# q and k stored whole and parted by GpSimd in attention's first chunk, with three edits in the last layer

## The chip, the cores and the metric

The kernel runs on one core of one Trainium2 chip. The core has TensorE (matrix products; PE in the profile), VectorE (DVE), ScalarE (ACT), GpSimd (POOL) and SyncE (SP), which here only issues transfers. Each takes its own instructions in order; they wait for one another through semaphores. The metric is the device time of one launch in microseconds. Times "at" a number are counted from the start of the profiled span.

## The reference

A graph network of four layers on 3327 nodes with 128 features, and a random adjacency matrix of zeros and ones with about 16 neighbours per node. Every layer computes `x = x + layer(relu(layernorm(x)), adj)`:

- Layer 0: two rounds of `swish(adj @ h @ W + b)`.
- Layer 1: attention with 128 heads of 8 numbers each. q, k and v are raw reshapes of `h @ W.T` to (128, 3327, 8), so that one head's 3327 x 8 numbers come from about 26 consecutive nodes. The scores are `q k.T * 128**-0.5 + 2 adj`, then a softmax over the 3327 columns, the product with v, and an output projection.
- Layer 2: `relu(adj @ h @ W_msg)` through a gated recurrent cell.
- Layer 3: `z = leaky_relu(lap(adj, h) @ W1 + b1)`; all 3327 x 3327 squared distances between rows of z; for every row, the four nearest get `exp(-distance / 2)` added to the adjacency, and `lap(adj', h) @ W2 + b2` is the output, where `lap(A, x) = d * (A @ (d * x))`, d the inverse square root of the row sums.

## The kernel before, in words

Nodes lie on 128 partitions, 26 to a partition (N = 3327 nodes, T = 26, padded to NP = 3328). A matrix of nodes is walked in T tiles of 128 rows.

**Projection (lines 376 to 445).** After the layernorm and 26 transposes, a loop over r takes 128 nodes at a time: six products of 128 x 512 give 1024 numbers of q, k and v. For q and k, ScalarE writes the high part, the value rounded to the short fp32r format (L409), VectorE writes what is left over, the low part (L410), and takes the largest absolute value (L411). High and low part lie side by side in the tile `qk_st`, and SyncE stores both into the DRAM tensors `qt` and `kt`, whose 16 rows are 8 rows of high and 8 rows of low parts (L412). v is stored with a column of ones into `vd` (L419). At r == 1 the heads of group 0 are loaded (L421). Stores, loads and buffers in this part are ordered by the scheduler of the tile framework.

**Attention (lines 466 to 564).** The columns are cut into 7 chunks of 476 (`QW`), and the 128 heads into 32 groups of 4. The work is written out by hand as 7 x 32 x 26 steps (`manual_schedule`): every engine, SyncE included, takes its instructions in the order in which the steps issue them. A step t of a group does, in this order:

- `scores` (L483): four products of 32 x 128 by 32 x 476, one per head on its own row group of TensorE; to some heads the adjacency is added on VectorE (L499), to one on TensorE (L497), and in odd steps one head is taken without it, `exp` on ScalarE (L500) and then multiplied on GpSimd by `exp` of the adjacency (L502). In odd steps ScalarE takes the exponential of the five other results of the pair (L504).
- `weigh` (L506) of the step four before (`ahead = 4`): products with v, summed over the steps in one PSUM bank; at the end of a group the sum is copied (L520) and stored (L523).
- at t == 4, `load_heads` (L346) for the next group: 28 transfers on SyncE, 8 of keys into the one buffer `k_in` (`bufs=1`), 16 of queries, 4 of values.
- from t == 13, `key_pair` (L368): GpSimd copies the keys of two tiles into the order that TensorE reads.
- at t == 22, the adjacency tile of the next chunk: a load on SyncE and a doubling on GpSimd (L270), and a store of an older one (L481).

**After attention: `tail` (lines 586 to 829).** Output projection; `adj_product` for layer 2 in 26 tiles (L228, three bf16 parts of y on TensorE; the adjacency tiles `a16` are loaded from `adj16` through a pool opened for each product); the gates; `adj_product` for layer 3, z and its norms; then for each of 26 tiles the distances: 14 instructions of fp32 products (L774), 7 products of three rows that add the other rows' norms (L777), ScalarE's copy with the own norm (L778), VectorE's eight largest values and their places (L779, L780). `second` (L749) turns these into weights in pieces of 4, 9 and 13 tiles. While the third `adj_product` runs, `gather` (L787) fetches for each tile the four nearest rows of y from DRAM, one indirect transfer of GpSimd each, 104 in all, and VectorE weighs and adds them (L798, L800); TensorE transposes the sums (L805). At the end the product and the gathered sums are multiplied by W2 (L822, L823), scaled, added to x and stored.

At the very end a loop that runs `n_gen` times, 0 or 1, holds a general path for inputs on which the fast path isn't safe. `n_gen` is computed after the projection.

Of the kernel before, what the change touches and what calls it, by code (L numbers as in the profile page):

```python
# [8 lines left out]
F32 = mybir.dt.float32  # L9
F32R = mybir.dt.float32r  # L10
# [10 lines left out]
P = 128  # L21
# [5 lines left out]
E = 8  # L27
# [26 lines left out]
def kernel(  # L54
# [56 lines left out]
    deg = const.tile([P, T], F32, name="deg")  # L111
    a_max = const.tile([P, T], F32, name="a_max")
# [21 lines left out]
    def in_pieces(f):  # L134

        todo = [slice(t0, t1) for t0, t1 in zip(CUTS, CUTS[1:]) if t1 > t0]

        def done(t):
            while todo and todo[0].stop <= t:
                p = todo.pop(0)  # L140
                f(p, p.stop - p.start)

        return done
# [47 lines left out]
    def adj_matmul(agg, lhs, on_tile=None, bufs=3):  # L191

        cs = chunks(N, 512)
        with tc.tile_pool(name="adj_ps", bufs=1, space=PSUM) as ps, tc.tile_pool(name="adj_in", bufs=bufs) as ap:
# [23 lines left out]
    def adj_matmul_parts(agg, parts, on_tile=None):  # L218

        cs = chunks(N, 512)  # L220
        with tc.tile_pool(name="adj_ps", bufs=1, space=PSUM) as ps, tc.tile_pool(name="adj_in", bufs=4) as ap:
            acc = [ps.tile([P, 512], F32, name=f"agg_ps{c}") for c in range(len(cs))]
            for t in range(T):
                a = ap.tile([P, N], BF16, name="a16")
                nc.sync.dma_start(a, adj16[t])
                for i, part in enumerate(parts):
                    for c, (c0, w) in enumerate(cs):
# [5 lines left out]
                            stop=(t == T - 1 and i == 2),  # L233
# [39 lines left out]
    with tc.tile_pool(name="l0", bufs=1) as pool:  # L273
# [46 lines left out]
        fix = pool.tile([P, 1], F32, name="fix")  # L320
        nc.gpsimd.affine_select(fix, ones, pattern=[[0, 1]], compare_op=ALU.is_gt, fill=0.0, base=P - 1, channel_multiplier=-1)
        nc.vector.tensor_scalar(fix, fix, -1.0, 1.0, op0=ALU.mult, op1=ALU.add)
        nc.vector.tensor_add(deg[:, T - 1 : T], deg[:, T - 1 : T], fix)
# [4 lines left out]

    kt = dpool.tile([HL, GP], F32, name="kt")
# [15 lines left out]

    def load_heads(c, g):  # L346
        q0, _ = q_chunks[c]
        we = even(c)
        k_in = kq.tile([P, NP], F32, name="k_in", bufs=1)
        q4 = kq.tile([P, QW], F32R, name="q4")  # L350
        v4 = kq.tile([P, 4, T, EA], F32, name="v4")
        for i in range(4):
            n0 = (4 * g + i) * N
            for j in range(2):
                r = 32 * i + HL * j
                nc.sync.dma_start(k_in[r : r + HL], kt[:, n0 : n0 + NP])
                for k in range(2):
                    nc.sync.dma_start(
                        q4[r + E * k : r + E * k + E, :we].bitcast(F32),
                        qt[E * j : E * j + E, n0 + q0 : n0 + q0 + we],  # L360
                    )
# [14 lines left out]
    with tc.tile_pool(name="l1", bufs=1) as pool, tc.tile_pool(name="l1_ps", bufs=3, space=PSUM) as ps:  # L376
# [6 lines left out]
        for tail in (qt, kt):  # L383
            nc.gpsimd.dma_start(tail[:, N * NH :], zero)
# [12 lines left out]
        assert 3 * N + NP <= P * NH  # L397
        for r in range(T):
            kp = rows_of(r)
            lhs = hT[:, r * P : r * P + kp]  # L400
            for i, (dst, mx) in enumerate(((qt, q_max), (kt, k_max))):
# [3 lines left out]
                scale = D**-0.5 if i == 0 else 1.0  # L405
                s = st.tile([P, 2, E * NH], F32R, name="qk_st")
                full = pp[:kp].rearrange("p a b -> p (a b)")
                hi = s[:kp, 0].bitcast(F32)
                nc.scalar.activation(s[:kp, 0], full, AF.Copy, scale=scale)  # L409
                nc.vector.scalar_tensor_tensor(s[:kp, 1], full, scale, hi, op0=ALU.mult, op1=ALU.subtract)  # L410
                nc.vector.tensor_reduce(mx[:kp, r : r + 1], hi, AX.X, ALU.max, apply_absolute_value=True)  # L411
                store(dst.rearrange("e (r c) -> r e c", c=NH), s.bitcast(F32).rearrange("p a (e c) -> p (a e) c", c=NH), r, kp)  # L412
# [7 lines left out]
            if r == 1:  # L420
                first = load_heads(0, 0)  # L421
                while len(first[3]) < T // 2:
                    key_pair(first)
                e_first = [exp_of(a, 0) for a in a_first[1::2]]
# [15 lines left out]
        general = pool.tile([P, 1], F32, name="general")  # L440
# [515 lines left out]
```

## Time and profile before

| what | us |
| --- | --- |
| median of 3 runs | 11397.28 (11396.15 to 11406.29) |
| the profiled execution | 11392.72 |
| its span, first to last instruction | 11391.0 |
| layer 0 and layernorm, 0 to 382 | 382 |
| projection, to the first group's start at 641 | 259 |
| attention, 641 to 10592 | 9951 |
| output projection, to 10687 | 95 |
| layer 2, to 10861 | 174 |
| layer 3, first product, to 10974 | 113 |
| z and norms, to 11007 | 33 |
| distances, to 11215 | 208 |
| last weights, second product and gathers, to 11360 | 145 |
| last products and output, to 11391 | 31 |

The stages are cut at instructions in the order of time; the rows from 0 to 11391 sum to the span. A line of a timeline gives the start, the duration, the engine, the line of the code, the operation, output and inputs, and how many instructions were merged; in brackets stands how long the engine stood idle before it and what released it. A group line gives the count, then the busy time and the mean of one in ns, then the idle time just before, by releaser. A line of stretches gives start and end, the length, busy time and count of PE, PEld (weight loads), DVE, ACT and POOL, the granted clock of TensorE, the share of the DMA engines' time, and GB/s.

### The profile page before, as it was taken

What the parts mean: (1) busy time and instruction counts of PE and PEld (TensorE: products, weight loads), DVE (VectorE), ACT (ScalarE), POOL (GpSimd) and SP (SyncE); (2) the same over time, 40 slices, a digit from 0 to 9 for tenths busy, and PEclk for the clock granted to TensorE, in tenths of its full rate; (3) what the DMA queues carried; (4) which work ended last, traced back from release to release, by engine and by line L of the source; (5) the groups of instructions that cost most, each with busy time, mean ns of one, the idle gap of its engine ahead of it and who ended that gap; (6) DMA issues with size and microseconds to landing.
All of it is one profiled execution on the core that took longest, in us unless ns stands there. A gap on an engine that the chain in (4) does not pass through costs nothing. (4 is left out here: it accounts for less than half of the span.)

```text
span 11391.0 us, 212068 instructions
## 1 busy us (share of the span) xinstructions
PE 11065.1 (97%) x80100; PEld 3098.6 (27%) x80100; DVE 9408.1 (83%) x15508; ACT 10238.7 (90%) x9182; POOL 5727.5 (50%) x6218
## 2 busy tenths in 40 slices
PE   9789999999999999999999999999999999999998
PEld 4322222222222222222222222222222222222554
DVE  8678888888888888888888888888888888888555
ACT  0379999999999999999999999999999999999332
POOL 0135555555555555555555555555555555555103
PEclk9899999999999999999999999999999999999999
DMA  7853444444444444444444444444443434444423
GB/s 268 244 122 60 70 62 67 64 62 69 61 69 63 63 68 61 69 63 63 67 61 69 63 61 67 61 68 63 62 68 60 68 57 58 58 57 59 138 79 114
DMA packets 476579, 889.80 MB, mean 78 GB/s; under 512 B 91863, under 2 KB 423112, under 8 KB 439962
## 3 DMA queue, kind: packets, MB, share of 16 engines
q1 hardware_dynamic: 470952, 864.64, 43.5%
q8 instruction: 633, 10.37, 0.5%
q0 software_dynamic: 4592, 11.50, 0.3%
q14 instruction: 402, 3.29, 0.1%
HBM read 763.30 MB, written 112.46 MB: 77 GB/s over the span
## 5 line engine op out<-in xcount | busy, mean ns | idle before, releaser
L499 DVE TENSOR_TENSOR p<-early,a 128x476 f32<-128x476 f32 (+1 forms) x14560 | 8435.6, 644 | 1419.7 <-PE early L494 1192.3
L504 ACT ACTIVATE p<-p 128x2380 f32<-128x2380 f32 (+1 forms) x2912 | 6757.4, 2321 | 14.2 <-DVE p L499 0.5
L511 PE MATMUL acc<-p,v 128*9 128x476 f32 (+1 forms) x46592 | 5879.6, 564 | 33.4 <-POOL p L502 13.6
L502 POOL TENSOR_TENSOR p<-p,e 128x476 f32<-128x476 f32 (+1 forms) x2912 | 3539.2, 1215 | 3296.0 <-ACT p L500 3259.4
L500 ACT ACTIVATE p<-late 128x476 f32<-128x476 f32 (+1 forms) x5824 | 4529.2, 897 | 38.9 <-DMA vd<-v_st 20.3
L494 PE MATMUL early<-q,k 32*128 32x476 f32 (+1 forms) x14560 | 2882.9, 477 | 18.8 <-DVE p L499 18.8
L494 PE MATMUL late<-q,k 32*128 32x476 f32 (+1 forms) x8736 | 2797.3, 478 | 62.7 <-ACT p L500 36.3
L373 POOL CAST k<-k_in 128x256 fp32r<-128x256 f32 x2912 | 1946.7, 703 | 1162.5 <-DMA q<-qt 582.7
L494 PEld LDWEIGHTS late<-q,k 32*128 32x128 f32 x8736 | 1065.4, 181 | 4769.9 <-ACT p L500 3241.0
L497 PE MATMUL late<-a,two_i 128*128 128x476 bf16 (+1 forms) x5824 | 2181.0, 374 | 0.0
L494 PEld LDWEIGHTS early<-q,k 32*128 32x128 f32 x14560 | 1144.9, 181 | 23.9 <-DVE p L499 19.5
L511 PEld LDWEIGHTS acc<-p,v 128*9 128x9 f32 x46592 | 710.6, 88 | 1406.4 <-issue 1185.1
L497 PEld LDWEIGHTS <-two_i 128*128 128x128 bf16 x5824 | 556.3, 96 | 1327.5 <-issue 1327.5
L187 ACT COPY agg<-agg_ps 128x512 f32<-128x512 f32 x15 | 8.2, 590 | 476.7 <-PE agg_ps L201 289.7
L228 PE MATMUL agg_ps<-a,part 128*128 128x512 bf16 (+1 forms) x1638 | 338.0, 368 | 18.1 <-DMA a<-adj 13.7
L270 POOL TENSOR_SCALAR a<-a_in 128x476 bf16<-128x476 f32 (+2 forms) x156 | 222.2, 1424 | 0.5
L228 PEld LDWEIGHTS <-part 128*128 128x128 bf16 x1638 | 161.7, 99 | 188.6 <-DVE d_half L759 13.7
L409 ACT ACTIVATE qk_st<-pp 128x1024 fp32r<-128x1024 f32 (+1 forms) x52 | 53.3, 1024 | 149.0 <-DMA qt<-qk_st 67.4
L270 POOL TENSOR_SCALAR a<-a 128x476 bf16<-128x476 f32 (+1 forms) x26 | 36.4, 1400 | 295.3 <-DMA a<-in_adjT_dram 295.3
L778 ACT ACTIVATE dist<-sp,nsq 128x2048 f32<-128x2048 f32 (+1 forms) x52 | 85.5, 1647 | 109.8 <-PE sp L777 100.8
L774 PE MATMUL sp<-yT,hT 128*128 128x512 f32 (+1 forms) x364 | 168.2, 603 | 3.6 <-ACT hT L726 2.1
L201 PE MATMUL agg_ps<-a,h 128*128 128x512 f32 (+2 forms) x364 | 147.4, 568 | 24.3 <-DVE h L162 24.3
(192 smaller groups left out, 2520.2 us busy)
## 6 DMA issues: line engine op xcount, KB each, us to landing
k_in<-kt SPq DMA_DIRECT2D x1792, 208.0 KB
v<-vd SPq DMA_DIRECT2D x896, 117.0 KB
a<-in_adjT_dram SPq DMA_DIRECT2D x50, 1663.5 KB
a<-adj SPq DMA_DIRECT2D x78, 831.8 KB
q<-qt SPq DMA_DIRECT2D x3072, 14.9 KB
a_in<-in_adjT_dram SPq DMA_DIRECT2D x125, 238.0 KB
qt<-qk_st SPq DMA_DIRECT2D x25, 1024.0 KB
kt<-qk_st SPq DMA_DIRECT2D x25, 1024.0 KB
```

Of the source, the lines that this page charges most:

```text
L201: nc.tensor.matmul(acc[c][:, :w], lhs[:kp, t, :], a[:kp, c0 : c0 + w], start=(t == 0), stop=(t == T - 1))
L228: nc.tensor.matmul(acc[c][:, :w], part[:, t, :], a[:, c0 : c0 + w], start=(t == 0 and i == 0), stop=(t == T - 1 and i == 2),)
L270: nc.gpsimd.tensor_scalar(a2[:kp, :w], a, 2.0, None, op0=ALU.mult)
L373: nc.gpsimd.tensor_copy(k, slots(k_in)[:, t : t + 2, :])
L494: nc.tensor.matmul(sp[:, :we], pairs[t // 2][r, t % 2, :], q4[r, :we], start=True, stop=ways[i] != "I")
L497: nc.tensor.matmul(late[:, i - n_d, :we], two_i, a2[:, :we], start=False, stop=True)
L499: nc.vector.tensor_tensor(p8[:, places[i], :we], early[i][:, :we], a2[:, :we], op=ALU.add)
L500: nc.scalar.activation(p8[:, places[n_d] : places[3] + 1, :we], late[:, :, :we], AF.Exp)
L502: nc.gpsimd.tensor_tensor(p8[:, places[3], :we], p8[:, places[3], :we], e_a[:, :we], op=ALU.mult)
L504: nc.scalar.activation(p8[:, :5, :we], p8[:, :5, :we], AF.Exp)
L511: nc.tensor.matmul(acc[32 * i : 32 * i + EA, :w], v4[:kp, i, t, :], p8[:kp, PLACES[t % 2][i], :w], start=(t == 0), stop=(t == T - 1),)
L774: nc.tensor.matmul(sp[:, c0 : c0 + w], slots(zT)[:, t, :], z2T[:, cols], start=True, stop=False)
```

## The change

- In the projection q and k are stored whole, one 1024-column tile `qk_st` each, into new tensors `qf` and `kf`. The low part on VectorE is gone.
- A class `Parting` makes the two parts of a group's k and q. For each side it loads the four heads' numbers as 96 partitions of 1109 columns into `lo_k` or `lo_q`; `part` then lets GpSimd, in four pieces of 278 columns, cast them to fp32r into a tile named `hi` and subtract that in place from the loaded tile; `store` writes both into `kt` or `qt`. Groups 0 and 1 are parted inside the projection, one item of a list `early` per row r; `load_heads(0, 0)` is moved from r == 1 into that list, behind them. From there on group g of the first chunk parts group g + 2: the k side in steps 2 to 5 with its store at step 7, the q side in steps 9 to 12 with its store at step 14; the loads for group g + 3 are at step 20.
- `load_heads` loads N columns of keys and w of queries and clears the padding by a memset on GpSimd.
- Layer 3: `h @ W2` is computed beside the first product (`project_quad`), and y is made from it, so that the last product needs no weights but only transposes. The nearest row of the four is taken from y in place, not gathered, and the gathered sum is added straight to x. Whether the nearest row was each row itself is checked on VectorE and joins `n_gen` at the end. The norm products use four row groups (rows 0, 32, 64, 96) in turn. The adjacency pool stays open over all products; the distance tiles use the buffers `ln_xc` and `agg`. `second` has a fourth piece: 4, 9, 9 and 4 tiles.
- The general path reads `kf` and `qf` instead of adding the parts.

```diff
+    JW = 12
+    WJ = 4 * N // JW
+    W4 = -(-WJ // 4)
+    SIDES = ((kf, kt, "lo_k"), (qf, qt, "lo_q"))
+    class Parting:
+        def __init__(self, g):
+            self.g, self.hi, self.lo = g, [None] * 2, [None] * 2
+        def rows(self, ap, r):
+            return dram(ap, r * GP + 4 * self.g * N, [[GP, E], [WJ, JW], [1, WJ]])
+        def load(self, side):
+            src, _, name = SIDES[side]
+            self.lo[side] = kq.tile([E * JW, WJ], F32R, name=name, bufs=1)
+            nc.sync.dma_start(self.lo[side].bitcast(F32), self.rows(src, 0))
+        def part(self, side, i):
+            if i == 0:
+                self.hi[side] = kq.tile([E * JW, WJ], F32R, name="hi", bufs=1)
+            p = slice(i * W4, min((i + 1) * W4, WJ))
+            hi, lo = self.hi[side][:, p], self.lo[side][:, p]
+            nc.gpsimd.tensor_copy(hi, lo.bitcast(F32))
+            nc.gpsimd.tensor_sub(lo, lo.bitcast(F32), hi.bitcast(F32))
+        def store(self, side):
+            dst = SIDES[side][1]
+            nc.sync.dma_start(self.rows(dst, 0), self.hi[side].bitcast(F32))
+            nc.sync.dma_start(self.rows(dst, E), self.lo[side].bitcast(F32))
+        def at(self, t):
+            for side, t0 in ((0, 2), (1, 9)):
+                if t0 <= t < t0 + 4:
+                    self.part(side, t - t0)
+                if t == t0 + 5:
+                    self.store(side)
...
-                s = st.tile([P, 2, E * NH], F32R, name="qk_st")
-                full = pp[:kp].rearrange("p a b -> p (a b)")
-                hi = s[:kp, 0].bitcast(F32)
-                nc.scalar.activation(s[:kp, 0], full, AF.Copy, scale=scale)
-                nc.vector.scalar_tensor_tensor(s[:kp, 1], full, scale, hi, op0=ALU.mult, op1=ALU.subtract)
-                nc.vector.tensor_reduce(mx[:kp, r : r + 1], hi, AX.X, ALU.max, apply_absolute_value=True)
...
+                s = st.tile([P, E * NH], F32, name="qk_st")
+                nc.scalar.activation(s[:kp], pp[:kp].rearrange("p a b -> p (a b)"), AF.Copy, scale=D**-0.5 if i == 0 else 1.0)
+                nc.vector.tensor_reduce(mx[:kp, r : r + 1], s[:kp], AX.X, ALU.max, apply_absolute_value=True)
+                store(dst[:E].rearrange("e (r c) -> r e c", c=NH), s.rearrange("p (e c) -> p e c", c=NH), r, kp)
...
                 if t == min(4, T // 2) and more:
                     coming = load_heads(*groups[n])
+                if c == 0 and g + 2 < n_groups:
+                    if t == 0:
+                        parting = ahead_part
+                    for due in range(t, t + 1 if t < T - 1 else max(T, 21)):
+                        parting.at(due)
+                        if due == 20 and g + 3 < n_groups:
+                            ahead_part = Parting(g + 3)
+                            ahead_part.load(0)
+                            ahead_part.load(1)
...
+                            r = slice(c0 // 16, c0 // 16 + 3)
-                            nc.tensor.matmul(sp[:, c0 : c0 + w], one_rows, n_rows[:, cols], start=False, stop=True)
+                            nc.tensor.matmul(sp[:, c0 : c0 + w], one_rows[r], n_rows[r, cols], start=False, stop=True)
...
+                    if k == 0 and not general:
+                        row = y[:, t, :]
+                    else:
+                        row = gpool.tile([P, D], F32, name="row")
...
-                        nc.tensor.matmul(op[:, j, :], slots(agg)[:, t0 + j, :], w2_s, start=True, stop=False)
-                        nc.tensor.matmul(op[:, j, :], gT[:, t0 + j, :], w2_s, start=False, stop=True)
+                        nc.tensor.transpose(op[:, j, :], slots(agg)[:, t0 + j, :], ident)
```

## The prediction

> **What bounds the kernel now.** I read first the page's forty slices and its costliest groups: from 641 to 10592 us the span is attention, 224 groups of 26 steps (7 chunks of columns by 32 groups of four heads). Then I read the order of time of each engine in a few groups of the first chunk, and the busy times of the stages around it.
>
> ```profile
> L504 ACT ACTIVATE p<-p 128x2380 f32<-128x2380 f32 (+1 forms) x2912 | 6757.4, 2321 | 14.2 <-DVE p L499 0.5
> L502 POOL TENSOR_TENSOR p<-p,e 128x476 f32<-128x476 f32 (+1 forms) x2912 | 3539.2, 1215 | 3296.0 <-ACT p L500 3259.4
> L373 POOL CAST k<-k_in 128x256 fp32r<-128x256 f32 x2912 | 1946.7, 703 | 1162.5 <-DMA q<-qt 582.7
> ```
>
> ScalarE sets the pace: it is hardly ever idle, and two steps take 3.385 us (26 steps, 44.0 us). TensorE is close behind (1.64 us a step, 3.28 a pair). GpSimd looks half empty, and its long idle times are waits, for ScalarE and, at L373, for transfers. The order of time of one group (step 0 near 730.7 us) shows why:
>
> ```profile
> 738.04 1.38 SPq L523 DMA_DIRECT2D ot<-o  x4
> 739.52 0.33 SPq L356 DMA_DIRECT2D k_in<-kt  x1
> ...
> 755.39 0.32 SPq L356 DMA_DIRECT2D k_in<-kt  x1
> ...
> 757.22 0.35 SPq L362 DMA_DIRECT2D v<-vd  x1
> 757.86 0.35 SPq L481 DMA_DIRECT2D adj<-a  x1
> ```
>
> ```profile
> 748.03 1.22 POOL L502 TENSOR_TENSOR p<-p,e 128x476 f32<-128x476 f32 x1 [2.17 <-ACT p L500]
> ...
> 754.80 1.21 POOL L502 TENSOR_TENSOR p<-p,e 128x476 f32<-128x476 f32 x1 [2.17 <-ACT p L500]
> 761.50 1.35 POOL L373 CAST k<-k_in 128x256 fp32r<-128x256 f32 x2 [5.50 <-DMA q<-qt]
> 762.77 1.25 POOL L502 TENSOR_TENSOR p<-p,e 128x476 f32<-128x476 f32 x1
> ```
>
> ```profile
> 756.30 0.98 PE L511 MATMUL acc<-p,v 128*9 128x476 f32 x8
> ...
> 763.06 1.98 PE L511 MATMUL acc<-p,v 128*9 128x476 f32 x8
> ```
>
> The 28 transfers of `load_heads`, written at step 4, hold SyncE's queue from 739.5 to 757.6, some 18 us or eleven steps; even the adjacency store written at step 22 goes out at 757.86, the moment the queue is free. GpSimd takes its work in order too: at step 13 it waits until 761.5 for the keys, 6.1 us after the last key transfer was issued, and the product of step 15 comes late, so that TensorE's `weigh` at 763.06 takes 1.98 us for 0.98. That costs next to nothing, as TensorE runs some 2 us ahead of ScalarE. (Step 15's scores are at 755.57; the `weigh` at 756.30 is that of step 11, four steps back.)
>
> Before attention, the projection is bound by transfers, at 301 GB/s with the DMA engines full:
>
> ```profile
> 428.00:620.00 192.00, 134.22 (x256) 49.22 (x256) 101.25 (x88) 65.27 (x66) 11.16 (x28) 0.91 1.04 301
> ```
>
> **The change part by part.** All sums stand against the profiled execution, 11392.7 us (span 11391.0); the median shown, 11397.3, is 4.6 above it.
>
> *Projection, q and k stored whole: -50 us.* A row takes 8.97 us for 1024 + 1024 + 576 KB; without the low parts it is 1600 KB, 5.46 us at the same rate, while TensorE needs 12 x 0.43 = 5.15 and ScalarE 3 x 1.02. 26 rows x 3.5 = -91. Added there: the parting of groups 0 and 1 (0.85 MB loaded, 1.70 stored, each) and the first loads of group 2, 6.0 MB or 20 us. GpSimd's four partings (8 instructions of 0.72 = 5.8 us a side, priced below) are waited for on SyncE, with the row stores behind them: from nothing, if the backlog covers them, to 4 x (5.8 + 6.1 for a landing) = 47. I take 20, nearer the lower end, because backlog stands at every row. The removed L410 (52 x 1.22 on VectorE) is worth nothing: transfers cover it. Bounds -80 to -20.
>
> *First chunk, parting on GpSimd: +371 us.* Price of one: a cast of 278 columns by L373 (0.67 us for 256 when back to back) is 0.73, a subtraction by L502 (1.21 for 476) 0.71; a side is 4 of each, 5.75 us, a group 11.5. As work that fits: GpSimd is busy 25 of 44 us. The order does not fit. Both sides write their high part to the one buffer named `hi` (`bufs=1`), so the first cast of the q side, at step 9, has to wait until the k side's `hi` has been stored and has landed. That store is written at step 7, behind `load_heads` of step 4 on SyncE's queue. Its data are ready early (steps 2 to 5, done near 745), but the queue is free only at 757.6. The landing: 6.1 us for a key transfer of 208 KB in that backlog, so 416 KB issued at 758 is there near 763.5. Meanwhile GpSimd, in order, stands from 749.25 (product of step 9 done) to 763.5. Behind the waiting cast are the two partings of steps 9 and 10 (2.9 us) and then the product of step 11: done at 767.6. TensorE wants it at 756.3 and stands 11.3 us; with it stand VectorE and ScalarE, which empty what is begun. The product of step 13 follows two more partings, at 771.7; after that GpSimd catches up (2.55 us a pair against 3.385).
>
> What the group loses: TensorE resumes at 767.6. With its usual durations ScalarE takes up step 20 near 778.1 instead of 766.53. It will not have its usual clock: after the 19 us idle before 641 its scores take 0.76 us for 0.48 and the first 44 us have a granted clock of 0.86 against 1.00 later. About 5 us of such work adds 1.5. So 13.1, less 0.3 that the wait at step 13 costs now: 12.8 a group. Group 0 is spared (its loads start before its first step), groups 30 and 31 part nothing: 29 x 12.8 = 371. From both sides: with the smallest landing shown (2.4 us, from the last `nd` store to the load that waits on it) plus 1.5 for 416 KB at 301 GB/s the cast starts at 761.9, 11.2 a group, 325; with a landing of 10 at 768, 17, 495. SyncE's later work (the q side's stores wait for GpSimd until about 771, then the next loads, then the adjacency tile of step 22, due near 780) still comes in time; if it did not, the slack is TensorE's four steps, 6.7 us.
>
> The Trainium skill, in "DMA: Bandwidth & Descriptors", section "Anatomy of one DMA", puts a transfer at about 2.0 us fixed plus bytes by 436 GB/s. By that rule the store would be there 3.0 us after issue, at 761, a group would lose about 10.3, and the sum would be lower by 73. The trace's 6.1 us under backlog is what I use, since this store goes out behind the same backlog.
>
> The cut of `k_in` to N columns and two memsets of one column (0.13 us): nothing, in GpSimd's idle time; without that cover 224 x 0.13 = 29 us of GpSimd.
>
> *Tail: -37 us.* (a) h w2 beside layer 3's first product: TensorE fills that product (111.8 of 113 us), so 26 transposes (0.11 each, L646) and 52 matmuls (0.234, L718) add +15. (b) Norm rows on four row groups: a distance tile takes TensorE 7.82 us, of it 1.03 + 0.71 for L777; in parallel some 0.5 (attention's four row-group scores end 0.49 us after they begin), and VectorE's 3.63 + 0.09 + 3.62 = 7.36 with a small gap becomes the bound: 26 x 0.46 = -12, +2 for the small instructions of a fourth piece. (c) The last piece is 4 tiles for 13: gathers start 4 us earlier. (d) 78 gathers for 104 at 1.249: -32. TensorE's last product (111.7) then becomes late next; it starts after the last distance tile, as its adjacency tiles are loaded ahead and the first pieces are ready. (c) and (d) together -33, at worst -20 if TensorE starts as late as now (11219.4). (e) Last stage: 26 transposes of 0.23 for 104 matmuls of 18.8 us in all; VectorE's 9.3 us takes over, -9. The reduction for `need` falls beside the output. Bounds -50 to -15.
>
> Sum: 11392.7 - 50 + 371 - 37 = 11676.7; against the median, about 11680 us.
>
> **The rivals.** (1) *The wait is hidden.* GpSimd's own work is short, and half its time is free; if the high part is free again by step 9, only gains are left: 11397 - 87 = 11310. For it: the data are ready 4 us before step 9. Against: eleven steps of queue. It decides where a group loses less than 87 / 29 = 3.0 us, so where the k side's store has landed by 753.7, before the last of the head loads is even issued. (2) *The wait is longer.* The k store writes the tensor that `load_heads` reads; if it waits also for those reads (761.5) it lands near 767: +3.5 x 29, 11780. Against: in the projection a row store goes out at 420.90, 0.2 us after the last such load was issued. (3) *Half of it.* Fewer bytes in the queue or a short landing, 4 to 8 us a group: 11450 to 11540. (4) *The nearest row is not the row itself* somewhere: then the general branch repeats attention, more than double the time; a row's distance to itself is zero but for rounding, so under 1%.
>
> **How the numbers follow.** Forecast 0.65 (its own range 11570 to 11780), (1) 0.13, (2) 0.12, (3) 0.09, mixtures within 0.2% 0.01. For the range I leave out (1) below and a little above: 11440 to 11820. Faster by over 0.2% is (1), 0.13; within 0.2%, about what a measurement can tell from no change, 0.02; slower 0.85.
>
> **What would show it.** GpSimd's cast of the parting with some 14 us idle before it, 29 times, ended by a `kt` store; TensorE's L511 waiting for the product of step 11, 11 us each; groups of the first chunk near 57 us, those of later chunks at 44; attention starting near 590 for 641; gathers 78, distance tiles at 7.4. I am wrong if the parting's store reaches the queue ahead of the loads, if the two sides hold separate buffers, or if the first chunk's groups stay at 44 us.

## The result, and the profile after

The kernel after takes 11738.8 us (median; 11715.3 to 11741.2) against 11401.8 for the kernel before, run beside it (11396.2 to 11406.6). The ratio is 1.0291, with a 95% interval from 1.0273 to 1.0309: slower, by 337 us. The profiled execution took 11737.6 us, span 11735.8, which is 344.8 more than the span of before. Those 344.8 us can be laid out by stage, each time read from the order of time of the two traces:

| stage | before | after | difference | forecast |
|---|---|---|---|---|
| start to the output store of the first group | 694.1 | 627.1 | -66.9 | -50 |
| first output store to the end of attention | 9898.1 | 10261.9 | +363.7 | +371 |
| end of attention to the end | 798.8 | 846.8 | +48.0 | -37 |

The two large terms came as forecast. The third has the wrong sign, and most of the experiments below were spent on it.

**First chunk.** The page's costliest groups of the kernel after show the new wait and the two engines that wait with it (busy time, mean ns of one, then the idle time before it and what ended it):

```profile
L567 PE MATMUL acc<-p,v 128*9 128x476 f32 (+1 forms) x46592 | 5929.0, 566 | 333.0 <-POOL p L558 312.7
L556 ACT ACTIVATE p<-late 128x476 f32<-128x476 f32 (+1 forms) x5824 | 4511.6, 891 | 384.1 <-PE late L553 371.5
L377 POOL CAST hi<-lo_q 96x278 fp32r<-96x278 f32 (+1 forms) x128 | 52.6, 413 | 426.6 <-DMA kt<-hi 397.5
```

Ahead of the 128 casts of the q side GpSimd stood idle 397.5 us for the landing of a store from `hi`; TensorE stood 312.7 us for GpSimd's products, and ScalarE 371.5 us for TensorE. In the order of time this wait stands before the first q cast of each of groups 1 to 29, 13.8 to 15.4 us each. One group gives the chain. First SyncE's queue (start, duration, what is issued):

```profile
1023.29 1.38 SPq L579 DMA_DIRECT2D ot<-o  x4
1024.77 0.31 SPq L405 DMA_DIRECT2D k_in<-kt  x1
...
1042.40 0.36 SPq L411 DMA_DIRECT2D v<-vd  x1
1043.05 0.71 SPq L382 DMA_DIRECT2D kt<-hi  x1
1044.33 0.66 SPq L383 DMA_DIRECT2D kt<-lo_k  x1
1054.25 0.64 SPq L382 DMA_DIRECT2D qt<-hi  x1
```

The k side's store goes out at 1043.05, the moment the last head load is issued; its data had been ready since 1028.3, as GpSimd's order of time shows:

```profile
1027.90 0.42 POOL L377 CAST hi<-lo_k 96x275 fp32r<-96x275 f32 x1
1028.40 0.77 POOL L378 TENSOR_TENSOR lo_k<-lo_k,hi 96x275 fp32r<-96x275 f32 x1
1029.88 1.22 POOL L558 TENSOR_TENSOR p<-p,e 128x476 f32<-128x476 f32 x1 [0.71 <-ACT p L556]
1033.27 1.22 POOL L558 TENSOR_TENSOR p<-p,e 128x476 f32<-128x476 f32 x1 [2.17 <-ACT p L556]
1049.04 0.41 POOL L377 CAST hi<-lo_q 96x278 fp32r<-96x278 f32 x1 [14.55 <-DMA kt<-hi]
...
1051.48 1.18 POOL L558 TENSOR_TENSOR p<-p,e 128x476 f32<-128x476 f32 x1
```

The q side's first cast waits 14.55 us until that store has landed, 6.0 us after its issue, and the product of step 11 comes at 1051.48, behind two pairs of casts and subtractions. TensorE is ready for it at 1042.5:

```profile
1041.54 0.98 PE L567 MATMUL acc<-p,v 128*9 128x476 f32 x6
1052.71 1.75 PE L567 MATMUL acc<-p,v 128*9 128x476 f32 x2 [10.19 <-POOL p L558]
1054.40 0.76 PE L550 MATMUL late<-q,k 32*128 32x476 f32 x1
```

Here one sees the stop (10.19 us) and the low clock behind it (0.76 us for 0.48; the granted clock from 1053 to 1057 is 0.57, and 1.00 again from 1057). Groups 1 to 29 take 56.5 us on average, 55.5 to 57.7, for 44.3 before, which is 355 us of the 363.7. From group 30 on a group takes 44.45 us for 44.41, which is the other 8.

**Tail.** From the end of attention the stages moved by +3.1 (output projection), +0.8 (layer 2's product), +15.8 (layer 3's first product, with h w2 beside it: 127.6 for 111.8), -9.2 (distances, 207.6 for 216.8), **+42.5** (from the end of the last FIND, VectorE's last search for the nearest rows, to TensorE's first instruction of the last stage: 190.0 for 147.5) and -4.3 (last stage); the rest is -0.6. The +42.5 is in TensorE's order of time in the last product:

```profile
11513.70 33.75 PE L232 MATMUL agg_ps<-a,part 128*128 128x512 bf16 x167 [1.43 <-ACT agg L879]
11548.29 0.27 PE L232 MATMUL agg_ps<-a,part 128*128 128x255 bf16 x1 [0.83 <-issue]
11551.07 0.38 PE L232 MATMUL agg_ps<-a,part 128*128 128x512 bf16 x1 [2.51 <-issue]
11553.88 0.59 PE L232 MATMUL agg_ps<-a,part 128*128 128x512 bf16 x1 [2.44 <-issue]
11556.67 0.58 PE L232 MATMUL agg_ps<-a,part 128*128 128x512 bf16 x1 [2.20 <-issue]
...
11640.89 69.39 PE L232 MATMUL agg_ps<-a,part 128*128 128x512 bf16 x336 [0.35 <-issue]
```

For 34 us the product runs at its full rate. Then a matmul comes every 2.8 us, and the weight load between two of them lies halfway: one instruction each 1.40 us. "issue" says that the profile shows nothing that TensorE waited for. From 11592 on the steps are uneven, 26 matmuls in 48 us. It goes on until 11640.9, 3 us after GpSimd's last gather was issued; then 336 matmuls run without a gap. I call these 92 us the slow stretch. What the engines did in it, by windows (busy time of TensorE, its weight loads, VectorE, ScalarE and GpSimd with their counts, then granted clock, DMA share and GB/s):

```profile
11513.00:11548.00 35.00, 33.75 (x167) 16.24 (x166) 20.11 (x40) 7.49 (x10) 20.14 (x18) 1.00 0.56 194
11548.00:11592.00 44.00, 8.41 (x16) 1.75 (x17) 14.85 (x45) 0.00 (x0) 30.26 (x32) 0.55 0.23 67
11592.00:11640.00 48.00, 14.44 (x26) 2.70 (x26) 16.79 (x53) 0.00 (x0) 31.31 (x33) 0.50 0.21 64
11641.00:11710.00 69.00, 69.00 (x335) 33.18 (x335) 3.15 (x9) 0.66 (x2) 0.00 (x0) 0.97 0.50 174
```

The DMA engines are at a fifth, and no engine is full: GpSimd, the busiest, is at 0.69 and 0.65. The low granted clock (0.50 to 0.55) explains a matmul of 0.58 us for 0.38, not an instruction every 1.40; it also comes later than the first gaps, for from 11548 to 11552 it is still 1.00. In the trace of before, the same product beside 104 gathers has no such gap:

```profile
11250.00:11333.00 83.00, 83.00 (x424) 41.53 (x423) 21.77 (x67) 5.54 (x21) 62.89 (x67) 1.00 0.67 223
```

### The profile page after: what moved, and what is told of

Read it like the earlier page. It is cut to its first block, busy times and chain, and to the rows that moved or that the text cites. A ratio compares the mean times of both kernels' runs of the same rounds, so it can differ in the third digit from the quotient of the medians.

```text
span 11735.8 us, 213042 instructions
## 1 busy us (share of the span) xinstructions
PE 11107.0 (95%) x80074; PEld 3098.1 (26%) x80074; DVE 9375.0 (80%) x15508; ACT 10243.6 (87%) x9163; POOL 6008.5 (51%) x6966
## 4 chain that ended last, share of the span: by engine, by line
PE 71%; DMA 11%; DVE 7%; issue 4%; POOL 3%; ACT 2%; SPq 1%; POOLq 0%; DVEq 0%; ACTq 0%
PE acc L567 35%; PE late L550 16%; PE late L553 11%; DMA q<-qt 5%; DVE p L555 5%; PE agg_ps L232 3%; PE agg_ps L205 2%; DMA v<-vd 2%; DMA k_in<-kt 2%; DMA kt<-hi 1%; POOL p L558 1%; PE early L550 1%; ACT p L556 1%; DVE o L576 1%; SPq L579 1%
## 5 line engine op out<-in xcount | busy, mean ns | idle before, releaser
L567 PE MATMUL acc<-p,v 128*9 128x476 f32 (+1 forms) x46592 | 5929.0, 566 | 333.0 <-POOL p L558 312.7
L556 ACT ACTIVATE p<-late 128x476 f32<-128x476 f32 (+1 forms) x5824 | 4511.6, 891 | 384.1 <-PE late L553 371.5
L550 PEld LDWEIGHTS early<-q,k 32*128 32x128 f32 x14560 | 1150.6, 182 | 15.4 <-DVE p L555 10.2
L377 POOL CAST hi<-lo_q 96x278 fp32r<-96x278 f32 (+1 forms) x128 | 52.6, 413 | 426.6 <-DMA kt<-hi 397.5
L576 DVE COPY o<-acc 105x476 f32<-105x476 f32 (+1 forms) x224 | 144.4, 645 | 4.6 <-PE acc L567 4.6
## 6 DMA issues: line engine op xcount, KB each, us to landing
q<-qt SPq DMA_DIRECT2D x3072, 14.9 KB
```

The costliest lines, as they stand in the source:

```text
L550: nc.tensor.matmul(sp[:, :we], pairs[t // 2][r, t % 2, :], q4[r, :we], start=True, stop=ways[i] != "I")
L556: nc.scalar.activation(p8[:, places[n_d] : places[3] + 1, :we], late[:, :, :we], AF.Exp)
L567: nc.tensor.matmul(acc[32 * i : 32 * i + EA, :w], v4[:kp, i, t, :], p8[:kp, PLACES[t % 2][i], :w], start=(t == 0), stop=(t == T - 1),)
L576: nc.vector.tensor_copy(o4[: 96 + EA, :w], acc[: 96 + EA, :w])
```

## The experiments: the first chunk

**Two buffers.** My theory was that the buffer `hi`, shared by the two sides, does the damage. The rival was the amount of new work on GpSimd and in the transfers.

```diff
-                self.hi[side] = kq.tile([E * JW, WJ], F32R, name="hi", bufs=1)
+                self.hi[side] = kq.tile([E * JW, WJ], F32R, name=("hi_k", "hi_q")[side], bufs=1)
...
-            a = a_pool.tile([P, QW], F32, name="a_in")
+            a = a_pool.tile([P, QW], F32, name="a_in", bufs=1)
...
-                o4 = a_pool.tile([P, QW], F32, name="o4")
+                o4 = a_pool.tile([P, QW], F32, name="o4", bufs=1)
```

> The k side and the q side of the parting get a rounded-part buffer each (room for it: a_in and o4, used about once a group, keep one buffer in place of two). Theory of the shared buffer (GpSimd's first cast of the q side waits for the landing of the k side's store): the 14.6 us wait of that cast goes, the groups of the first chunk return from about 57 us to 44 to 45 us, so about 29 x 12.5 = 360 us of the time after, 11738.8, come back: 11380, within 40. Rival, the work itself (about 10 us of casts and subtractions a group on GpSimd in front of the products of L558, and four more transfers of 0.4 MB a group): the groups stay over 52 us and less than 150 us come back. In between: the products of L558 still late by the few us that parting work stands before them, groups of 46 to 50 us.

Measured: 11472.4 us (11465.6 to 11481.7), ratio to before 1.0047 (1.0030 to 1.0064). Groups 1 to 29 take 46.6 us for 56.5. That is 9.9 of the 12.3 us that a group had lost, 287 us in all, and the wait at the q cast is gone in all 29 groups, so the shared buffer is shown. The tail is as in the kernel after (849.8 us, slow stretch included). The 46.6 us lie in the band that the expectation gave to products late behind the parting work; what is left, 2.4 us a group, spread from 43.9 to 49.6, has another name in this run's waits (engine and line, what was waited for: us in total, times, longest; 26 groups of the first chunk):

```profile
POOL a L274 <- DMA a_in<-in_adjT_dram: 82.6, 17, 5.6
```

GpSimd waits for the adjacency tile of the next chunk, once in most groups. In the kernel after, whose groups are longer, the same wait was 5.0 us in 21 groups. SyncE's order of time in one group says why the tile is late:

```profile
881.87 0.66 SPq L383 DMA_DIRECT2D kt<-lo_k  x1
882.62 0.78 SPq L382 DMA_DIRECT2D qt<-hi_q  x1
883.50 2.01 SPq L383 DMA_DIRECT2D qt<-lo_q  x1
888.18 0.70 SPq L370 DMA_DIRECT2D lo_k<-kf  x1
892.65 0.69 SPq L370 DMA_DIRECT2D lo_q<-qf  x1
893.40 0.46 SPq L537 DMA_DIRECT2D adj<-a  x1
893.91 1.32 SPq L174 DMA_DIRECT2D a_in<-in_adjT_dram  x1
```

The next parting is loaded into `lo_k` and `lo_q`, one buffer each, so each load waits on SyncE for the landing of its own store (881.87 to 888.18 and 883.50 to 892.65), and the load of `a_in` stands behind both. It is the first mechanism once more: a transfer that waits for a landing, at the head of a queue that is taken in order.

**The store before the loads.** The same theory from the other side: keep one buffer, and bring the store out early.

```diff
-            for side, t0 in ((0, 2), (1, 9)):
+            for side, t0, t1 in ((0, 0, 4), (1, 9, 14)):
                 if t0 <= t < t0 + 4:
                     self.part(side, t - t0)
-                if t == t0 + 5:
+                if t == t1:
                     self.store(side)
...
-                if t == min(4, T // 2) and more:
-                    coming = load_heads(*groups[n])
...
+                if t == min(4, T // 2) and more:
+                    coming = load_heads(*groups[n])
```

(The two lines of `load_heads` move behind the block that calls `parting.at`.)

> The buffer stays shared; the k side is parted two steps earlier (steps 0 to 3) and its store goes into SyncE's queue at step 4 ahead of the loads of the next heads, in place of step 7 behind them. Theory of the shared buffer behind the queue: the store lands about 6 us after its issue near step 5, before step 9 asks for the buffer, the wait of the cast is under 2 us and the groups of the first chunk come back to 44 to 46 us; time about 11380 to 11420. Rival, a write of the shared buffer waits for something else than this store (the second store from lo, or reads of the parted rows): the cast still waits over 8 us and the groups stay over 52 us. Rival of the work itself: groups over 52 us with no wait at the cast. A cost either theory has to pay: the next heads' loads are issued some us later, and the first k pairs (step 13) could wait up to 3 us a group.

Measured: 11565.8 us (11557.4 to 11582.3), ratio 1.0125 (1.0108 to 1.0142), groups of 50.2 us. The wait of the q side's cast is gone, in the group shown and in the other 28:

```profile
997.08 1.21 POOL L558 TENSOR_TENSOR p<-p,e 128x476 f32<-128x476 f32 x1 [2.18 <-ACT p L556]
998.24 0.41 POOL L377 CAST hi<-lo_q 96x278 fp32r<-96x278 f32 x1
...
1004.28 1.20 POOL L558 TENSOR_TENSOR p<-p,e 128x476 f32<-128x476 f32 x1
1013.57 1.27 POOL L422 CAST k<-k_in 128x256 fp32r<-128x256 f32 x2 [8.09 <-DMA v<-vd]
```

But the price that the expectation named came out larger than the 3 us given to it. Behind the stores the head loads take until 1009.8, and GpSimd waits 8.1 us for the keys, where it waited 5.5 in the group that the prediction shows. Both rivals fall: the cast waits for nothing, and 50.2 us is under the 52 that they asked for. But the groups miss the 44 to 46 us of the theory, for half of the gain goes into the next wait down the same queue.

**The order of the queue.** In the last two variants of the first chunk, both on two buffers, the load of `a_in` no longer stands behind a load that waits on SyncE for a landing. (The parting's loads still wait, for a store of `lo_q` 75.6 us in 24 groups, but behind `a_in`.) In the first the next parting's loads go behind the load of `a_in`; in the second they go at step 0 of the group that parts, with the k side parted at steps 5 to 8.

```diff
-                        if due == 20 and g + 3 < n_groups:
-                            ahead_part = Parting(g + 3)
-                            ahead_part.load(0)
-                            ahead_part.load(1)
...
+                if c == 0 and g + 3 < n_groups and t == 22:
+                    ahead_part = Parting(g + 3)
+                    ahead_part.load(0)
+                    ahead_part.load(1)
```

They ran in the kernels of the next section, and the expectations stand there. Measured in six profiles: groups 1 to 29 take 44.36 to 44.49 us on average in every one of them (44.27 in the kernel before), and the wait for `a_in` falls to 1.4 us in 27 groups (read with the first chunk alone repaired). GpSimd does all of its parting in these runs as well. So the work itself costs at most 0.2 us a group; the rest of the 12.3 us was waits for landings in SyncE's queue.

## The experiments: the slow stretch

**The check of the nearest rows.** The change put a reduction and an all-reduce over the partitions on GpSimd in front of the gathers, and SyncE's read of `n_gen` amid the product's loads (11530.9; 656.7 in the kernel before). Two kernels part these from the rest.

```diff
+        nc.vector.tensor_copy(n_gen, unsafe)
...
-            if not general:
-                need = pool.tile([P, 1], F32, name="need")
-                nc.vector.tensor_reduce(need, moved, AX.X, ALU.max)
-                nc.gpsimd.partition_all_reduce(need, need, P, bass_isa.ReduceOp.max)
-                nc.vector.tensor_max(need, need, unsafe)
-                nc.vector.tensor_copy(n_gen, need)
```

> The check of the nearest rows (moved, need and the partition all-reduce on GpSimd) is left out and n_gen is taken from the bounds alone right after the projection, as in the kernel before; that is, a set of nodes whose nearest row is not itself would not be sent to the general branch. Theory that the check causes the slow stretch of the last product (TensorE issues an instruction every 1.4 us from 17 us after the first gather until the last gather): the product runs at its full rate, TensorE's 546 matmuls in about 115 us from the first gather's wait on, the tail is 40 to 50 us shorter, time 11690 to 11700. Rival that the gathers without transposes and ScalarE's copies between them cause it: the stretch stays, time 11715 to 11740. The first chunk is as in the kernel after in both.

The second takes out the last removed line alone and adds the first:

> The check with its all-reduce on GpSimd stays where it is, but its result isn't used: n_gen is taken from the bounds right after the projection, so that SyncE reads it some 10.9 ms earlier than in the kernel after and not in the middle of the product's loads. Theory of the all-reduce (it leaves GpSimd in a state in which its gathers hold up the others): the slow stretch stays, time 11715 to 11740, and GpSimd's last drain stays near 8 us. Theory of SyncE's read amid the loads: the stretch goes, time 11690 to 11700. Rival that neither matters: as the first, and the run without the check is slow too.

Measured: 11761.8 (11746.8 to 11770.2) and 11771.3 us (11746.7 to 11780.0), ratios 1.0298 and 1.0301. From the last FIND to the last stage both take as long as the kernel after, 191.4 and 190.3 us, with the slow stretch from 14.5 and 16.4 us after the first gather (counted to the last matmul at full rate; 16.0 in the kernel after). Neither the all-reduce nor the read amid the loads is the cause. GpSimd's last drain takes 8.07 us in both, as in the kernel after, against 1.30 before, so that isn't the all-reduce either. In the kernel after it ends some 5 us later than SyncE's own, which is the gain that the last stage lacks (-4.3 for -9).

**Four edits of the last product.** Each undoes or moves one thing that the change did to it, on the repaired first chunk. Back in come the transposes of the gathered sums and their copies by ScalarE:

```diff
+            def transpose_gathered(t):
+                tp = g_ps.tile([P, P], F32, name="tp")
+                nc.tensor.transpose(tp, gs[t], ident)
+                nc.scalar.copy(gT[:, t, :], tp)
...
-                adj_product(agg, y, parts, gather)
+                adj_product(agg, y, parts, beside)
+                for t in range(max(T - LAG, 0), T):
+                    transpose_gathered(t)
```

(`beside(t)` gathers for tile t and transposes the sum of tile t - 6; nothing reads the copies.)

> On two buffers (as in the run with two buffers), with two edits in places that don't touch. First chunk: the next parting's loads go into SyncE's queue at step 22, behind the load of a_in, in place of step 20 ahead of it. Theory that the rest of the first chunk's loss (46.6 us a group for 44.3) is GpSimd waiting at L274 for a_in, whose load stands on SyncE behind loads that wait for the landing of the parting's stores: groups of 44.3 to 45.2, 40 to 65 us back. Rival that the rest is GpSimd's own work in front of the products of L558: groups stay at 46 to 47. Last product: TensorE transposes each gathered sum and ScalarE copies it (to a tile that nothing reads), as the kernel before did, six tiles late. Theory that the slow stretch needs an idle ScalarE and a TensorE that does nothing but the product: it goes, the stretch from the last FIND to the last stage falls from 190 us to 125 to 150. Rival, the nearest row in place of a gather or the update of xs on VectorE: it stays at 180 us or more.

The node's own row scaled by ScalarE:

```diff
-                        nc.vector.tensor_scalar_mul(g, row, sim[:, t, 0:1])
+                        nc.scalar.activation(g, row, AF.Copy, scale=sim[:, t, 0:1])
```

> First chunk as in the run with the transposes back: same expectations. Last product: ScalarE in place of VectorE scales the node's own row (L906), so that ScalarE has one instruction a tile and VectorE one less; no transposes. Theory of the idle ScalarE: the slow stretch goes, the stretch from the last FIND to the last stage falls from 190 us to 115 to 130. Theory that TensorE's own transposes with their waits keep the stretch away: it stays at 180 us or more. Theory that VectorE's read of y in place starts it: it goes too, and then the run with four gathers must show it gone as well.

The node's own row gathered again:

```diff
-                    if k == 0 and not general:
+                    if False:
                         row = y[:, t, :]
```

> On two buffers. First chunk: the parting's loads go at step 0 of the group that parts, the k side at steps 5 to 8 and the q side at 9 to 12, so that no load waits on SyncE for a landing: groups of 44.3 to 45.2 by the theory of the queue before a_in, 46 to 47 by the rival of GpSimd's own work. Last product: the node's own row is gathered like the three others (104 gathers in place of 78), the rest of the last product as in the kernel after. Theory that the nearest row in place causes the slow stretch: it goes, and the stretch from the last FIND to the last stage is set by the gathers, 104 x 1.25 + 15 = 145 us for 190. Rival that the missing transposes and ScalarE copies cause it: it stays and lasts as long as the gathers do, 104 x 1.37 = 143 us, in which TensorE does 40 matmuls less per 50 us, 215 to 225 us in all.

The update of `xs` taken out of the product's steps:

```diff
-                g = gpool.tile([P, D], F32, name="g")
+                g = g_all[:, t, :]
...
-                nc.vector.scalar_tensor_tensor(xs[:, t, :], g, d2[:, t : t + 1], xs[:, t, :], op0=ALU.mult, op1=ALU.add)
...
+                    nc.vector.tensor_add(o[:, :n], op[:, :n], g_all[:, t0 : t0 + n, :])
...
```

> First chunk as in the run with four gathers. Last product: the update of xs (L909) is taken out of the product's steps; the gathered sums are kept in a tile and added in the last stage, as in the kernel before (VectorE 4 instructions a tile in place of 5, the last stage some 3 us longer). Theory that VectorE's fifth instruction starts the slow stretch: it goes, 190 us becomes 115 to 130. Rivals (transposes and copies, or the nearest row in place): it stays at 180 us or more.

Measured, all four on one chip, whose kernel before takes 11380.5 us (11367.4 to 11397.5):

| last product | time, us | ratio to before (95%) | last FIND to last stage, us |
|---|---|---|---|
| transposes back | 11329.2 | 0.9950 (0.9933 to 0.9967) | 112.9 |
| scale on ScalarE | 11330.5 | 0.9956 (0.9939 to 0.9973) | 113.8 |
| four gathers | 11354.7 | 0.9975 (0.9966 to 0.9985) | 145.7 |
| no update beside | 11334.8 | 0.9960 (0.9945 to 0.9974) | 111.5 |

The stretch is absent in all four. TensorE's product is over some time before the last stage there, and what the last stage waits for is VectorE behind the last gathers, as this wait of the run with the scale on ScalarE shows:

```profile
PE op L918 <- DVE agg L192: 14.9, 1, 14.9
```

No theory of one cause in the last product expects that, and the four had two other things in common, the repaired first chunk and the chip. So I ran these apart, on one further chip.

> Two buffers and the parting's loads behind the load of a_in, and the tail exactly as in the kernel after. Four runs with one edit each in the last product lost the slow stretch, four with the product untouched had it, and those two sets were also run at different times. Theory that any of the four edits cures it: here it is there, 190 us from the last FIND to the last stage, and the kernel ends within 20 us of before. Theory that the order of the first chunk (the only thing that all four cured runs share) cures it, or the chip that they ran on: the stretch is absent, 110 to 125 us, and the kernel is 50 us or more faster than before. Groups of the first chunk 44.3 to 45.2 in either case.

> The kernel after with one edit: ScalarE scales the node's own row in the last product (L906); the first chunk is untouched, one buffer, groups near 57 us. Theory that the edit cures the slow stretch: 110 to 125 us from the last FIND to the last stage for 190, the time 65 to 75 us under the kernel after on this chip. Theory of the first chunk's order: it stays at 180 us or more. Theory of the chip: as the run of the unchanged kernel after beside it.

> The kernel after, unchanged, on the same chip as the other two. Theory that the slow stretch belongs to the program: it is there again, 1.4 us an instruction on TensorE from about 16 us after the first gather, 190 us from the last FIND to the last stage. Theory that it belongs to the chip that the first runs fell on: it is absent here, 110 to 125 us.

Measured: 11409.3 us (11402.7 to 11421.9; ratio 0.9994, 0.9985 to 1.0004) for the repaired chunk with the tail untouched; 11753.6 (11739.7 to 11760.7; ratio 1.0294) for the scale on ScalarE alone; 11753.8 in the one run of the kernel after. From the last FIND to the last stage they take 189.9, 189.7 and 189.7 us. The stretch is there in all three, from 15.6 to 16.1 us after the first gather. The repaired first chunk and the scale on ScalarE each leave it in place here, and the kernel that had both was without it on the chip of the four. The run with the scale on ScalarE also removes the theory of the idle ScalarE, for it has work all through the stretch:

```profile
11583.55 0.40 ACT L906 ACTIVATE g<-y,sim 128x128 f32<-128x128 f32 x1 [3.40 <-DVE g L908]
11587.24 0.40 ACT L906 ACTIVATE g<-y,sim 128x128 f32<-128x128 f32 x1 [3.29 <-DVE g L908]
11590.98 0.40 ACT L906 ACTIVATE g<-y,sim 128x128 f32<-128x128 f32 x1 [3.34 <-DVE xs L909]
```

The last run took the kernel with the transposes to one chip more, unchanged.

> The kernel of the run with the transposes back, unchanged, once more, on the chip that it falls on. The runs so far: the slow stretch in the kernel after, in two buffers alone, the store before the loads, no check, the check unused, the first chunk alone and the scale on ScalarE alone, on three chips; absent in the four runs that were made on one fourth chip, among them the scale on ScalarE with the first chunk's order, whose two parts are each slow alone elsewhere. Theory that the chip decides and the edits don't matter: on a chip other than that fourth one the stretch is here as well, 180 us or more from the last FIND to the last stage, and the time is that of the kernel before within 0.3%. Theory that TensorE's transposes and ScalarE's copies keep it away on any chip: 100 to 125 us, and the time 50 us or more under the kernel before. On the fourth chip again it would be absent by both.

Measured: 11365.9 us (11347.6 to 11375.5) against 11425.5 for before, ratio 0.9948 (0.9931 to 0.9966). From the last FIND to the last stage: 141.7 us, for 112.9 with the same program on the other chip. Neither expectation fits. TensorE's order of time here:

```profile
11218.23 3.83 PE L232 MATMUL agg_ps<-a,part 128*128 128x512 bf16 x17
11223.37 0.38 PE L232 MATMUL agg_ps<-a,part 128*128 128x512 bf16 x1 [1.30 <-issue]
11226.18 0.38 PE L232 MATMUL agg_ps<-a,part 128*128 128x512 bf16 x1 [2.43 <-issue]
11228.97 0.37 PE L232 MATMUL agg_ps<-a,part 128*128 128x255 bf16 x1 [2.41 <-issue]
11251.70 0.48 PE L897 MATMUL tp<-ident,g 128*128 128x128 f32 x1 [22.36 <-ACT ln_sq L898]
11251.97 5.74 PE L232 MATMUL agg_ps<-a,part 128*128 128x512 bf16 x21
11257.55 0.27 PE L897 MATMUL tp<-ident,g 128*128 128x128 f32 x1
11257.66 4.38 PE L232 MATMUL agg_ps<-a,part 128*128 128x512 bf16 x20
```

And ScalarE's first copy:

```profile
11251.38 0.27 ACT L898 COPY ln_sq<-tp 128x128 f32<-128x128 f32 x1 [44.40 <-remote]
```

The stretch begins as in the others, 15.6 us after the first gather, with three matmuls at the pace of 2.8 us. Then TensorE stands at its second transpose, because ScalarE makes the first copy 33 us after its transpose was done (11218.4), and the trace names what released it only as remote. From that copy on, TensorE runs at its full rate, with 70 us of gathers still to come. The same program on the chip of the four has none of this:

```profile
11186.00:11219.00 33.00, 32.05 (x157) 15.76 (x161) 18.63 (x34) 7.79 (x11) 18.69 (x16) 1.00 0.64 212
11219.00:11298.00 79.00, 78.58 (x395) 39.55 (x402) 33.05 (x103) 5.22 (x19) 59.80 (x64) 1.00 0.68 221
```

What is shown: the trace names nothing in the program that TensorE waits for in the stretch, and under one and the same program it came on one chip and not on another (29 us apart in this part of the tail). Where it came with the transposes it left 28 us of gaps on TensorE instead of 69 to 74. Each chip was used at one time only, so the chip can't be told from whatever else differed between those times. What isn't shown is its cause, nor that the transposes are what cut it short, since the tail without them was not run on that chip; nor was the tail of the kernel after ever run on the chip of the four. In the nine profiles that have the stretch it starts 14.5 to 16.4 us after the first gather. The version that beats both kernels, by 0.5%, is this one (two buffers, the loads behind `a_in`, the transposes back): 0.9950 and 0.9948 of the time before on two chips, without the stretch and with part of it. That the ratios agree although this program is 37 us slower on the second chip means that the kernel before was slower there as well, 11425.5 us for 11380.5; no trace of it was taken on either, so whether it has a stretch of its own there stays open.

## Why the prediction was right, point by point, and where it was not

- **The sum.** Forecast 11680 us, slower; measured 11738.8. Two of the three terms carry it; the third missed by 85 us. That the total is off by only 59 is in part luck, for the other two came out 17 and 7 us lower than forecast.
- **Parting, +371.** Measured +363.7. The mechanism is as put, step by step: the store at the queue's end, the landing 6.0 us after issue for the 6.1 taken, the q side's cast idle 14.55 us for 14, the product of step 11 behind two partings, TensorE's stop of 10.2 us for 11.3, the low clock after it. A group lost 12.3 us for 12.8, in 29 groups as forecast. The fit that the prediction cites from the Trainium skill ("DMA: Bandwidth & Descriptors", section "Anatomy of one DMA") is given there for transfers that GpSimd issues. It makes 3.0 us of this store, which SyncE issued behind 28 loads and which took 6.0; the measured row was the right one to take. That an edit on either side of the mechanism, the buffer or the place of the store, takes the cast's wait away shows that it was the cause. Two prices were off: a cast of 278 columns is 0.41 us, not the 0.73 taken from the key copies of L373, and the subtraction 0.77 for 0.71. Together a pair is 1.18 for 1.44, so the two pairs ahead of step 11's product took 0.5 us less than forecast. The sentence that SyncE's later work "still comes in time" held for this kernel (5.0 us of waits for `a_in` in 21 groups), and only because the groups were long: with the first wait gone, that work was the next bound, 2.4 us a group.
- **Projection, -50.** Measured -66.9 up to the first group's output. Without the 20 us set aside for SyncE's waits on GpSimd's early partings the sum is -71, which is nearer. SyncE did wait on GpSimd there, 4.2 us for the partings and 28.5 us for its work on `v_st`, so which of this was hidden by the transfers is open.
- **Tail, -37: this is the step that failed.** (a) +15 came as +15.8 and (b) as -9.2 for the distances, where -10 was forecast. (c) started TensorE's product early, at 11513.7, 7.8 us before the end of the last FIND. But "TensorE's last product (111.7) then becomes late next" took for granted that the product keeps the rate it has in the trace of before. It took 196.6 us, of which 92 in the slow stretch: +42.5 instead of -33 for (c) and (d). On the chip without the stretch the number comes out: with the scale on ScalarE the part from the last FIND to the last stage is 113.8 us for 147.5, -33.7. But the path is another than forecast. The product took 109.7 us there and ended 14.9 us before the last stage, which waited for VectorE behind the 78 gathers; so that -33.7 lies near -33 is in part luck. (e) gave -4.3 for -9, for GpSimd's last drain.
- **The rivals.** (1), the wait hidden, priced at 87 us of gain, is what the repaired first chunk gives, but no kernel gained as much: 26 to 51 us in the four on the chip without the stretch, and 4 us with the tail untouched and the stretch there. (2), a store that waits for the reads of `kt` as well, is refuted: the store went out 0.65 us after the last load was issued (1042.40 and 1043.05). (3) did not occur, though with one edit (the store before the loads) a group loses 6.0 us, by another wait. (4) did not occur either, for the general branch did not run.

## What to carry to other kernels

A shared buffer cost no wait at the cast here when its store went out ahead of the loads, and 14 us when it went out behind 28 of them in an in-order queue: GpSimd's 5 us of parting a side became 12 us a group for every engine. Before moving a store, list what is written ahead of it on its queue and who waits for its landing; then do it again for the next transfer behind it, since each repair here uncovered the next one. And a stage that is priced from a trace of one chip, with a neighbour removed, is an extrapolation: give it a bound on the side of a loss too.

## What the hardware did that I had not expected

In nine of the thirteen profiles of the changed kernel and its variants, TensorE went down to one instruction per 1.40 us at first, for up to 92 us beside GpSimd's gathers, while the DMA engines were at a fifth of their time. VectorE and GpSimd fell into the same steps later: in the kernel after two of VectorE's instructions start 2.80 us apart at 11576.98 and 11579.78, and GpSimd's gathers, at 1.25 us each until then, start at 11583.52, 11586.32 and 11587.72. The four profiles without it are those of four variants on one chip. No run tells why.
